# Edge records in two arrays, with the first 32 slots of each tile filled first, and keys and fields made in chunks of 120 columns

## The chip, the cores and the metric

One core of one Trainium2 chip runs the whole kernel in one launch. The metric is the device time in microseconds (us) of that core. The kernel is one program; its trace shows five engines: PE (matmul), DVE (vector), ACT (scalar), POOL (GpSimd) and SP (which issues transfers). "PEld" is PE's weight load. The core has 16 DMA engines that all transfers share. Transfers can be issued from the queues of SP and ACT, and from POOL, which issues the indirect ones.

## The reference, cut to what matters

A graph of 6250 nodes with 64 features, and 206250 directed edges sorted by target (100000 drawn edges in both directions, and one loop on each node). Four layers follow each other, each behind a layer norm and a ReLU, with a residual sum:

```python
h = relu(layernorm(x)); x = x + attention(h, edges)            # softmax over each node's edges, then a layer norm
h = relu(layernorm(x)); x = x + graph_conv(h, edges)           # sum over neighbours, scaled by degree
h = relu(layernorm(x)); x = x + message_net(h, edge_attr_64)   # two MLPs an edge, both directions
h = relu(layernorm(x)); x = x + gated_gnn(h, edge_type_4)      # 4 steps: sums by edge type, a GRU cell
```

All four sum over the same edges, so the kernel sorts the edges once into dense tiles and uses the tiles in all layers.

## The kernel before, in words

**Tiles and slots.** Nodes are padded to 49 blocks of 128 (`NB`), taken in 7 groups of 7 (`NG`, `GB`). A tile belongs to one group of target blocks and one source block, and a fiftieth tile of each group takes what a loop-laden diagonal pair has too much: `NC` = 50, so 350 tiles. A tile has `W` = 896 slots, 128 for each of its seven target blocks. Each slot holds a record of 70 floats (280 B): six fields and 64 edge features. All slots lie in the DRAM array `rec_d`; behind them it has one place an edge for those that find no room ("aside"). A slot's number is built from the pair of blocks (`base`) and the edge's rank within its pair, which counts on through all columns of edges. Slots that get no edge must hold -1 in their first four fields and zeros, so the array is filled before any record is written.

**Preparation (lines 189 to 251).** Edges lie as 128 partitions x 1620 columns (`EC`). The keys `dst`, `src` and the type are loaded whole. ACT issues seven fills of `rec_d` (line 215), each over 128 partitions. Meanwhile DVE makes from the keys: block numbers `bd` and `bs`, the fields `cf`, the pair's `key`, and `base`. PE turns `key` and `bd` into rows, stored in `row_d`. Then `pre_norm` makes `h` for the first layer.

**Sorting (`order`, to 2387 us in the trace).** Columns are taken in 162 groups of ten (`G`). The order of instructions on PE, ACT, DVE and SP is the one written out (`manual_schedule`). In iteration i: `load(i + 2)` issues three loads on SP, rows of keys `kr` (line 308), rows of block numbers `br` (line 310) and edge features into `rec` (line 312); `count(i + 1)` counts pairs on PE; `room_of(i + 1)` spreads what is left of each pair to the edges, after `br` is in; `settle(i)` works out rank and slot `pos` on DVE and then POOL issues ten indirect writes, one a column of 128 records (line 359). There are nine buffers for `rec` and ten for `pos`. Between these lie the projections of the first layer for iterations 0 to 13 (`projected`, with stores `q_d` and `v_d` on SP), and the attention scores after (`weights`, with a store on ACT).

**What reads the records.** The building of tiles (its own `load`, line 547: a tile's records `r`, and the scores `e`) makes count matrices `ak_d`; the message net (its `load`, line 928) reads the records again, beside rows `lid_d` and a table `pc`. A tile's records come as 128 partitions of 7 records, partition p holding the slots of rank p. When building ends a group, it stores 350 list rows to `lid_d` in writes of 128, 128 and 94 rows (line 631). A list of edges without room is worked off only if there are any.

Of the kernel before, what the change touches and what calls it, by code (L numbers as in the profile page):

```python
# [8 lines left out]
F32 = mybir.dt.float32  # L9
F32R = mybir.dt.float32r  # L10
F16 = mybir.dt.float16
# [3 lines left out]
I32 = mybir.dt.int32  # L15
AF = mybir.ActivationFunctionType
OP = mybir.AluOpType
AX = mybir.AxisListType

P = 128  # L20
D = 64
K = 4
# [4 lines left out]
class Plan:  # L27
# [7 lines left out]

    def __init__(self, n_nodes, n_edges, gb=7, group=10):
        self.N, self.E = n_nodes, n_edges
        nb = -(-n_nodes // P)
        self.NG = -(-nb // gb)
        self.GB = -(-nb // self.NG)  # L40
        self.NB = self.NG * self.GB
        self.NC = self.NB + 1
        self.NP = self.NB * P
        self.W = self.GB * P
        self.NSLOT = self.NG * self.NC * self.W
        self.G = group
        self.EC = -(-n_edges // (P * group)) * group
        self.EP = self.EC * P
        assert self.NB <= P and self.NB * self.NB <= 4094
        assert self.NSLOT + self.EP < 1 << 24 and K * self.NP < 1 << 24  # L50
        assert self.G * self.NB <= 512 and 512 < self.W <= 1024 or self.NG == 1
# [3 lines left out]
def gnn_stack(ctx: ExitStack, tc: tile.TileContext, pl: Plan, a: dict, out: bass.AP):  # L55
    nc = tc.nc
    NB, NC, NG, GB, W = pl.NB, pl.NC, pl.NG, pl.GB, pl.W
# [40 lines left out]
    nc.sync.dma_start(x, a["x"].rearrange("(b p) d -> p b d", p=P))  # L98
# [3 lines left out]
    rec_d = dram.tile([pl.NSLOT + pl.EP, RW], F32, name="rec_d")  # L102
    rec_v = rec_d[: pl.NSLOT, :].rearrange("(t p j) r -> t p j r", p=P, j=GB)
# [9 lines left out]
    e_d = dram.tile([NG * NB, P, W], F32, name="e_d")  # L113

# [18 lines left out]
    def pre_norm(pool):  # L133
        normalize(h, x, pool)
        nc.vector.tensor_scalar(h, h, 0.0, None, op0=OP.max)
# [46 lines left out]
    with ExitStack() as st:  # L182
# [3 lines left out]


        cf = sp.tile([P, EC, RF], F16, name="cf")
        nc.vector.memset(cf[:, :, 4], 1.0)
# [10 lines left out]
        nc.vector.tensor_scalar(minus, ident[:NB, :NB], -1.0, None, op0=OP.mult)  # L200

        with tc.tile_pool(name="prep", bufs=1) as pp:
            keys = {}
            for n in ("dst", "src", "ety"):
                keys[n] = pp.tile([P, EC], I32, name="k_" + n)
                nc.sync.dma_start(keys[n], a[n])

            many = max(f for f in (1, 2) if NC % f == 0)
            fill = sp.tile([P, many * GB, RW], F32, name="fill")
            nc.vector.memset(fill, 0.0)  # L210
            nc.vector.memset(fill[:, :, 0:4], -1.0)
            fill_v = rec_d[: pl.NSLOT, :].rearrange("(p i j) r -> p i (j r)", p=P, j=many * GB)
            per = NC // many
            for i in range(NG):
                nc.scalar.dma_start(fill_v[:, i * per : (i + 1) * per, :],
                                    fill.rearrange("p j r -> p (j r)")[:, None, :]
                                    .to_broadcast([P, per, many * GB * RW]))
            ti = pp.tile([P, EC], I32, name="ti")
            bf = pp.tile([P, EC], F32, name="bf")
            for n, b in (("dst", bd), ("src", bs)):  # L220
                nc.vector.tensor_scalar(ti, keys[n], 7, None, op0=OP.arith_shift_right)
                nc.vector.tensor_copy(b, ti)
            nc.vector.tensor_copy(bf, bd)
            for f, n in ((0, "dst"), (1, "src")):
                nc.vector.tensor_scalar(ti, keys[n], P - 1, None, op0=OP.bitwise_and)
                nc.vector.tensor_copy(cf[:, :, f], ti)
            for f, m, s in ((3, P - 1, 1), (5, 1, 0)):
                nc.vector.tensor_scalar(ti, keys["dst"], m, s, op0=OP.bitwise_and, op1=OP.arith_shift_right)
                nc.vector.tensor_copy(cf[:, :, f], ti)
            nc.vector.scalar_tensor_tensor(cf[:, :, 2], keys["ety"], float(P // 2), cf[:, :, 3],  # L230
                                           op0=OP.mult, op1=OP.add)
            nc.vector.tensor_scalar(cf[:, :, 5], cf[:, :, 5], 255.0, 1.0, op0=OP.mult, op1=OP.add)
            nc.vector.scalar_tensor_tensor(key, bd, float(NB), bs, op0=OP.mult, op1=OP.add)
            nc.vector.tensor_scalar(key, key, -float(NB * NB // 2), None, op0=OP.add)

            with tc.tile_pool(name="rowps", bufs=2, space=PSUM) as ps:
                for c0 in range(0, EC, P):
                    n = min(P, EC - c0)
                    pt = ps.tile([P, 2, P], F32, name="pt")
                    nc.tensor.transpose(pt[:n, 0, :], key[:, c0 : c0 + n], ident)  # L240
                    nc.tensor.transpose(pt[:n, 1, :], bf[:, c0 : c0 + n], ident)
                    rt = pp.tile([P, 2, P], F16, name="rt", bufs=3)
                    nc.vector.tensor_copy(rt[:n], pt[:n])
                    nc.sync.dma_start(row_d[:, c0 : c0 + n, :].rearrange("k t e -> t k e"), rt[:n])

            grp = pp.tile([P, EC], F32, name="grp")
            nc.vector.tensor_scalar(grp, bd, float(GB), None, op0=OP.is_ge)
            for k in range(2, NG):
                nc.vector.scalar_tensor_tensor(grp, bd, float(k * GB), grp, op0=OP.is_ge, op1=OP.add)
            nc.vector.scalar_tensor_tensor(base, bs, float(W), bd, op0=OP.mult, op1=OP.add)  # L250
            nc.vector.scalar_tensor_tensor(base, grp, float(NC * W - GB), base, op0=OP.mult, op1=OP.add)
# [10 lines left out]
        with tc.tile_pool(name="l0i", bufs=1) as wk:  # L262
            pre_norm(wk)

        sw = s2.enter_context(tc.tile_pool(name="sortw", bufs=3))
        ps = s2.enter_context(tc.tile_pool(name="sortps", bufs=2, space=PSUM))

# [34 lines left out]
        nc.gpsimd.iota(aside, pattern=[[1, G]], base=pl.NSLOT, channel_multiplier=EC,  # L302
# [22 lines left out]
        def settle(i, kr, rec, pr):  # L325
# [15 lines left out]
            nc.vector.scalar_tensor_tensor(pf, r, -float(GB), base[:, gs], op0=OP.mult, op1=OP.add)  # L341

            t1 = sw.tile([P, G], F32, name="t1")
            nc.vector.tensor_scalar(t1, bs[:, gs], -float(W), float((NB - 1) * W), op0=OP.mult, op1=OP.add)
            nc.vector.scalar_tensor_tensor(t1, r, -float(P), t1, op0=OP.is_le, op1=OP.mult)
            nc.vector.tensor_tensor(pf, pf, t1, op=OP.add)

            room = sw.tile([P, G], F32, name="room")
            nc.vector.tensor_tensor(room, bd[:, gs], bs[:, gs], op=OP.is_equal)
            nc.vector.tensor_scalar(room, room, -float(P - 1), -float(P), op0=OP.mult, op1=OP.add)  # L350
            ov = over[:, gs]
            nc.vector.tensor_tensor(ov, r, room, op=OP.is_le)
# [5 lines left out]
            for t in range(G):  # L358
                s = nc.gpsimd.indirect_dma_start(  # L359
                    out=rec_d, out_offset=bass.IndirectOffsetOnAxis(ap=pos[:, t : t + 1], axis=0),  # L360
                    in_=rec[:, t, :], in_offset=None)
                tc.declare_no_dep(s.ins, group="records", reason="each edge has its own slot")
                tc.add_to_no_dep_group("records", s.ins)

        def projected():

            for k, n0 in enumerate(range(0, pl.NP, 512)):
                n = min(512, pl.NP - n0)
                s = slice(n0, n0 + n)
                b0, nb = n0 // P, n // P  # L370
                hT = hTs[k % 2]
# [40 lines left out]
        def order():  # L412
            groups = EC // G
            ahead = [load(k) for k in range(min(2, groups))]
# [26 lines left out]
            for i in range(groups):  # L441
                share = scored(i)
                next(share, None)
                if i + 2 < groups:
                    ahead.append(load(i + 2))
                kr, _, rec = ahead.pop(0)
                if i + 1 < groups:
                    count(i + 1)
                next(share, None)
                nxt = room_of(i + 1, ahead[0][1]) if i + 1 < groups else None  # L450
                settle(i, kr, rec, pr)
                for _ in share:
                    pass
                pr = nxt
# [78 lines left out]
    with ExitStack() as st:  # L533
# [11 lines left out]
        def load(g, c):  # L545
            r = wk.tile([P, GB, RW], F32, name="r", bufs=4)
            nc.sync.dma_start(r, rec_v[g * NC + c])
            e = None
            if c < NB:
                e = wk.tile([P, W], F32, name="e", bufs=4)  # L550
                nc.sync.dma_start(e, e_d[g * NB + c])
            return r, e
# [320 lines left out]
    with ExitStack() as st:  # L873
# [4 lines left out]
        with ExitStack() as s1:  # L878
# [46 lines left out]
            def load(g, ci):  # L925
                t = g * NC + ci
                r = wk.tile([P, GB, RW], F32, name="r", bufs=3)
                nc.sync.dma_start(r, rec_v[t])
# [490 lines left out]
```

## Time and profile before

| | us |
|---|---|
| median of 10 runs | 9700.97 |
| lowest and highest | 9691.37, 9713.13 |
| the profiled execution's own time | 9684.43 |
| its span, first to last instruction | 9682.6 |
| first, 161st and last record write start | 250.38, 470.76, 2386.95 |
| building of tiles and the first layer's sum | 2387 to 3851 |
| message net, main loop | 4100 to 6910 |
| gated layer and end | 6910 to 9682 |

Over the span PE is busy 83%, DVE 77%, ACT 59%, POOL 30%, and the DMA engines move 1948.57 MB, 201 GB/s. The shares are means over stages with different limits; the windows of a stage say what limits it. A row of a window lists PE, PEld, DVE, ACT and POOL busy with their counts, then the granted PE clock, the mean busy share of the 16 DMA engines and the GB/s. Times of a row in the timeline are the start and the length; behind them stand engine, line, operation, what it writes and reads, and in brackets how long the engine was idle before and what ended that.

### The profile page before, as it was taken

What the parts mean: (1) busy time and instruction counts of PE and PEld (TensorE: products, weight loads), DVE (VectorE), ACT (ScalarE), POOL (GpSimd) and SP (SyncE); (2) the same over time, 40 slices, a digit from 0 to 9 for tenths busy, and PEclk for the clock granted to TensorE, in tenths of its full rate; (3) what the DMA queues carried; (4) which work ended last, traced back from release to release, by engine and by line L of the source; (5) the groups of instructions that cost most, each with busy time, mean ns of one, the idle gap of its engine ahead of it and who ended that gap; (6) DMA issues with size and microseconds to landing.
All of it is one profiled execution on the core that took longest, in us unless ns stands there. A gap on an engine that the chain in (4) does not pass through costs nothing. (4 is left out here: it accounts for less than half of the span.)

```text
span 9682.6 us, 146718 instructions
## 1 busy us (share of the span) xinstructions
PE 8048.1 (83%) x47524; PEld 6441.2 (67%) x47524; DVE 7486.0 (77%) x17172; ACT 5681.2 (59%) x8738; POOL 2877.2 (30%) x3651
## 2 busy tenths in 40 slices
PE   0564455453999999679999999999989999999999
PEld 0333333331444444568999999999768888888888
DVE  3697787774999998856777777777568888888888
ACT  0122122121666665546777777777568888888887
POOL 0777777776333332022222222222110000000000
PEclk9566666666999998879999999999989999999999
DMA  9565555554888886544444444444257777777777
GB/s 383 161 192 176 170 171 172 173 173 133 283 283 283 283 277 233 166 147 155 138 145 142 137 143 141 138 145 131 91 181 261 244 251 260 236 255 259 238 260 241
DMA packets 1035148, 1948.57 MB, mean 201 GB/s; under 512 B 327021, under 2 KB 579668, under 8 KB 1034214
## 3 DMA queue, kind: packets, MB, share of 16 engines
q1 hardware_dynamic: 748436, 1287.54, 41.4%
q10 hardware_dynamic: 224658, 564.27, 16.9%
q0 software_dynamic: 61248, 87.08, 2.7%
q8 instruction: 377, 6.18, 0.3%
q14 instruction: 429, 3.51, 0.1%
HBM read 1433.65 MB, written 504.81 MB: 200 GB/s over the span
## 5 line engine op out<-in xcount | busy, mean ns | idle before, releaser
L813 PE MATMUL ph<-mr,t 128*128 128x512 f32 x10976 | 2313.8, 370 | 9.6 <-DVE mr L799 8.1
L799 DVE CAST mr<-m 128x896 fp32r<-128x896 uint8 x3293 | 1954.0, 625 | 350.7 <-PE ph L813 244.4
L813 PEld LDWEIGHTS ph<-mr,t 128*128 128x128 f32 x10976 | 1991.2, 188 | 267.7 <-DVE mr L799 13.2
L797 ACT CAST mr<-m 128x896 fp32r<-128x896 uint8 x2195 | 1963.5, 940 | 309.1 <-PE ph L813 254.2
L359 POOL DMA_INDIRECT rec_d<-rec,pos x1620 | 1632.6, 1008 | 753.8 <-issue 437.2
L1062 DVE SCALAR_TENSOR_TENSOR m<-ph,m 128x512 fp32r<-128x512 f32 x1400 | 872.8, 623 | 423.0 <-ACT m L1061 390.6
L1078 POOL TENSOR_TENSOR acc_r<-acc_r,prc 128x128 f32<-128x128 f32 x784 | 610.8, 779 | 1799.4 <-ACT prc L1076 1768.7
L1061 ACT ACTIVATE m<-ph 128x512 fp32r<-128x512 f32 x1400 | 763.3, 545 | 572.3 <-PE ph L1054 530.7
L409 ACT ACTIVATE e<-e 128x896 f32<-128x896 f32 x343 | 323.9, 944 | 1244.7 <-DVE rec L357 310.7
L1054 PE MATMUL ph<-pc,st 128*128 128x256 f32 x4802 | 1008.1, 291 | 0.0
L1054 PE MATMUL ph<-qb,dt 128*128 128x256 f32 x4900 | 989.7, 284 | 0.0
L1054 PE MATMUL ph<-wc,eat 128*128 128x256 f32 x4900 | 988.8, 283 | 0.0
L599 ACT CAST ak<-pa 128x512 uint16<-128x512 f32 x1372 | 696.2, 534 | 387.7 <-PE pa L593 333.6
L1054 PEld LDWEIGHTS ph<-qb,dt 128*128 128x128 f32 x4900 | 762.0, 191 | 0.0
L1054 PEld LDWEIGHTS ph<-wc,eat 128*128 128x128 f32 x4900 | 758.7, 190 | 0.0
L1054 PEld LDWEIGHTS ph<-pc,st 128*128 128x128 f32 x4802 | 746.7, 192 | 8.1 <-DVE m L1062 6.3
L593 PE MATMUL pa<-kd,s 128*128 128x256 f16 x2401 | 687.6, 286 | 21.7 <-DVE kd L575 21.7
L1071 PE MATMUL pr<-m,so 128*128 128x260 f32 x2450 | 653.4, 285 | 22.1 <-ACT prc L1076 22.1
L293 PE MATMUL pc<-os,od 128*49 128x441 bf16 (+4 forms) x1619 | 374.1, 393 | 338.3 <-DVE os L270 337.7
L402 PE MATMUL pst<-qs,kt 128*128 128x512 f32 x1372 | 533.6, 533 | 135.3 <-DMA qs<-q_d 92.7
L1066 PE MATMUL pf<-m,do 128*128 128x256 f32 x2450 | 644.3, 281 | 0.0
L322 PE MATMUL pr<-y,dt 49*128 49x49 f16 x1620 | 90.1, 209 | 643.7 <-ACT y L296 598.9
(277 smaller groups left out, 13543.4 us busy)
## 6 DMA issues: line engine op xcount, KB each, us to landing
m<-ak_d SPq DMA_DIRECT2D x1372, 448.0 KB
r<-rec_d SPq DMA_DIRECT2D x700, 245.0 KB
e_d<-e ACTq DMA_DIRECT2D x343, 448.0 KB
e<-e_d SPq DMA_DIRECT2D x343, 448.0 KB
ak_d<-ak ACTq DMA_DIRECT2D x343, 448.0 KB
pc<-p_d SPq DMA_DIRECT2D x343, 256.0 KB
rec_d<-fill ACTq DMA_DIRECT2D x7, 12250.0 KB
rowst<-lid_d ACTq DMA_DIRECT2D x350, 224.0 KB
```

The source lines that it names most:

```text
L359: s = nc.gpsimd.indirect_dma_start(out=rec_d, out_offset=bass.IndirectOffsetOnAxis(ap=pos[:, t : t + 1], axis=0), in_=rec[:, t, :], in_off ...
L593: nc.tensor.matmul(pa, l_[:, j, :], r_[:, j, :], start=j % 2 == 0 and n == 0, stop=n + 1 == len(pairs), skip_group_check=True)
L599: nc.scalar.copy(ak2[:, :, (j + 1 - n) * HP : (j + 1) * HP].rearrange("p k (n q) -> p n k q", n=n), pa2[:, :n])
L797: nc.scalar.copy(m, src_t)
L799: nc.vector.tensor_copy(m, src_t)
L813: nc.tensor.matmul(ph[:, o : o + n], parts(c, k), r[:, o : o + n], start=(c == 0 and k == 0), stop=(c == NB - 1 and k == kk - 1))
L1054: nc.tensor.matmul(o, l_, r_, start=(q == 0 and j == j0), stop=(q == 5), skip_group_check=True)
L1061: nc.scalar.activation(mh, ph4, AF.Relu)
L1062: nc.vector.scalar_tensor_tensor(ml, ph4, 0.0, mh.bitcast(F32), op0=OP.max, op1=OP.subtract)
L1066: nc.tensor.matmul(pf[:, j], v["do"][:, j, :], m[:, j - j0, 0, : 2 * MSG], start=(ci == 0 and j % 2 == 0), stop=(ci == NB), skip_group_che ...
L1071: nc.tensor.matmul(pr, v["so"][:, j, :], m[:, j - j0, 1, :], start=(c is None or j == 0), stop=(c is None or j == GB - 1))
L1078: nc.gpsimd.tensor_tensor(acc_r[:, cb, :], acc_r[:, cb, :], prc[:, k * MSG : (k + 1) * MSG], op=OP.add)
```

## The change

- `rec_d` now has the places aside first and behind them two arrays of all slots. A record of rank under 32 (`R0`) goes to the first array, any other to the second; the fiftieth tile is all in the second.
- The fill comes in parts, with tiles on the outermost dimension (128, 128 and 94 of the 350): first the slots of rank under 32 in the first array (`fill_first`, three writes on ACT), then the others of the second array (`fill_others`), one write at the start of each of iterations 0 to 12: four quarters for each of the three sets of tiles, and the part of the fiftieth tiles.
- Groups 0 to 15 (`LEAD`, 160 columns) write to a slice of `rec_d` that ends with the first array; an edge of rank 32 or more would go aside there. From group 16 on the writes may go to all of `rec_d`. In the data no edge of the first 160 columns has a rank above 29.
- Keys and fields are made in 14 chunks of up to 120 columns: chunk 0 ahead of the loop, chunk k + 1 with its loads in iteration 12k + 1 and the rest in 12k + 3. The first norm is made in seven pieces as `projected` needs them.
- Both later loops load a tile's records with two transfers, 32 and 96 partitions (`load_records`).

```diff
+        self.R0 = P // 4
+        self.LEAD = max(1, self.EC // group // 10)
...
-    rec_d = dram.tile([pl.NSLOT + pl.EP, RW], F32, name="rec_d")
-    rec_v = rec_d[: pl.NSLOT, :].rearrange("(t p j) r -> t p j r", p=P, j=GB)
+    rec_d = dram.tile([pl.EP + 2 * pl.NSLOT, RW], F32, name="rec_d")
+    rec_p = [rec_d[pl.EP + k * pl.NSLOT : pl.EP + (k + 1) * pl.NSLOT, :] for k in range(2)]
+    rec_v = [r.rearrange("(t p j) r -> t p j r", p=P, j=GB) for r in rec_p]
+    rec_f = [r.rearrange("(t s) r -> t (s r)", s=W) for r in rec_p]
...
+    def load_records(r, t, ci):
+        if ci == NB:
+            nc.sync.dma_start(r, rec_v[1][t])
+        else:
+            nc.sync.dma_start(r[:R0], rec_v[0][t][:R0])
+            nc.sync.dma_start(r[R0:], rec_v[1][t][R0:])
...
+        many = 2
+        fill = sp.tile([P, many * GB * RW], F32, name="fill")
...
+        def fill_up(to, f):
+            n = to.shape[0]
+            to = to.rearrange("t (i e) -> t i e", e=many * GB * RW)
+            f.dma_start(to, fill[:n, None, :].to_broadcast(list(to.shape)))
+        def fill_first():
+            for t0 in range(0, NT, P):
+                fill_up(rec_f[0][t0 : min(NT, t0 + P), : R0 * GB * RW], nc.scalar)
+        def fill_others():
+            step = (P - R0) // 4 * GB * RW
+            for t0 in range(0, NT, P):
+                for q in range(4):
+                    o = R0 * GB * RW + q * step
+                    fill_up(rec_f[1][t0 : min(NT, t0 + P), o : o + step], nc.scalar)
+                    yield
+            fill_up(rec_p[1].rearrange("(g t s) r -> g t (s r)", t=NC, s=W)[:, NB, : R0 * GB * RW], nc.scalar)
+        fill_first()
...
-            fill_v = rec_d[: pl.NSLOT, :].rearrange("(p i j) r -> p i (j r)", p=P, j=many * GB)
-            per = NC // many
-            for i in range(NG):
-                nc.scalar.dma_start(fill_v[:, i * per : (i + 1) * per, :],
-                                    fill.rearrange("p j r -> p (j r)")[:, None, :]
-                                    .to_broadcast([P, per, many * GB * RW]))
...
+            if i < pl.LEAD:
+                nc.vector.tensor_scalar(ov, r, -float(R0), None, op0=OP.is_le)
+            else:
...
+                nc.vector.tensor_scalar(t1, r, -float(R0), float(pl.NSLOT), op0=OP.is_le, op1=OP.mult)
+                nc.vector.tensor_tensor(pf, pf, t1, op=OP.add)
...
-                    out=rec_d, out_offset=bass.IndirectOffsetOnAxis(ap=pos[:, t : t + 1], axis=0),
+                    out=rec_d[: pl.EP + pl.NSLOT, :] if i < pl.LEAD else rec_d, out_offset=...
...
+            keys = [load_keys(0)]
+            nc.sync.dma_start(x, a["x"].rearrange("(b p) d -> p b d", p=P))
+            prepare(0, keys.pop())
+            others = fill_others()
...
             for i in range(groups):
+                k, at = divmod(i, CH // G)
+                if k + 1 < len(chunks):
+                    if at == 1:
+                        keys.append(load_keys(k + 1))
+                    elif at == 3:
+                        prepare(k + 1, keys.pop())
+                next(others, None)
```

`prepare` does for 120 columns what the removed lines did for 1620, operation by operation, with its row store on SP; `load_keys` issues three loads on SP; `first_norm` does `pre_norm` for seven blocks at a time.

## The prediction

> **What bounds the kernel now.** I read the busy slices and the groups on the page first, then windows of the part that changes, then the timeline and the waits there. The change touches the sorting stage (to 2387 us) and the loads of records in two later stages. On the page, the scatters are 1620 indirect DMAs issued by POOL; the last starts at 2386.95 us, and the next stage reads what they wrote.
>
> ```profile
> L359 POOL DMA_INDIRECT rec_d<-rec,pos x1620 | 1632.6, 1008 | 753.8 <-issue 437.2
> ```
>
> From group 16 (scatter 160) on, one scatter starts every 1.313 us: 1008 ns busy and 0.30 us of "issue", in which POOL waits for nothing. The window says the same: 1471 us busy plus 1460 x 0.30 = 438 us make 1909 of its 1916 us. DVE has 490 us to spare in it, PE more. POOL sets the pace there, so what counts is when POOL begins. The columns are: window and length, then PE, PEld, DVE, ACT and POOL busy (count), PE clock, DMA share, GB/s.
>
> ```profile
> 10.00:249.00 239.00, 25.57 (x106) 14.28 (x106) 81.05 (x94) 6.41 (x11) 0.00 (x0) 0.95 1.02 390
> ...
> 470.80:2387.00 1916.20, 943.88 (x4312) 595.80 (x4311) 1426.31 (x5653) 381.93 (x475) 1471.32 (x1460) 0.65 0.52 169
> ```
>
> Up to 249 us the 16 DMA engines are full (share 1.02, 390 GB/s, so 24.4 GB/s an engine) with the fill: 7 x 12250 KB = 87.8 MB. ACT is held while issuing it, and the first scatter starts as it lands.
>
> ```profile
> 7.62 191.72 ACTq L215 DMA_DIRECT2D rec_d<-fill  x7
> ...
> 250.38 1.16 POOL L359 DMA_INDIRECT rec_d<-rec,pos  x1 [248.81 <-DMA br<-row_d]
> ```
>
> The releaser named here (br) is not it: the transfer records show the last fill packet at 248.8 us. In the first 160 scatters the pace is 1.378 us (470.76 - 250.38 over 160), a group of ten 13.8 us, and 14.4 over groups 4 to 11 (302.97 to 417.86 us).
>
> Two further views decide this case. SP's waits:
>
> ```profile
> SPq L310 <- DMA rec_d<-fill: 17.1, 1, 17.1
> ```
>
> A load of block rows (br) that has nothing to do with the fill waited for it. The trace shows why: issues from SP and ACT take eight semaphores in turn, and each waits until the transfer eight issues earlier has landed. And three writes of the later list rows (lid_d), two of 128 rows and one of 94, up to where other packets join; columns: length, PE clock, DMA share, GB/s:
>
> ```profile
> 2596.39:2596.78 0.39, 1.00 0.77 168
> 2597.93:2598.32 0.39, 1.00 0.77 168
> 2599.32:2599.99 0.67, 0.50 0.15 34
> ```
>
> The 94-row write, though smaller (47 against 64 KB), runs at a fifth of the rate. Its whole length is 1.57 us against 0.39, and in the transfer records a 128-row write ends with sixteen 4-byte packets, the 94-row one with two (3840.06 and 3840.07 us in the last group, where nothing else runs): it used two engines.
>
> **The change, part by part.** *The fill.* There are 350 tiles, and the new fills put tiles on the outermost dimension in pieces of 128, 128 and 94. The bytes hardly change. First part: 62,720 B a tile, so two writes of 8.03 MB and one of 5.90 MB. The rest: 47,040 B a tile in quarters, so eight writes of 6.02 MB, four of 4.42 MB, and a last one of 7 tiles (0.44 MB). A 128-tile piece runs at 390 GB/s: 20.6 us and 15.4 us. For a 94-tile piece there are two readings of the rows: by rate, a fifth of 390 (79 GB/s); by the end packets, two engines at 24.4 (48.8 GB/s). Small packets keep engines only partly busy, so the rate understates the gap for 3920 B packets; I take two engines: 121 us for the first part's piece, 90.6 us for each of the four others. The other reading gives 75 and 56 us, 46 + 138 = 184 us less in all; it stays as the lower end.
>
> *Start.* The first fill issues at about 8 us as now, its packets from 10. Two engines then have 41 + 121 us of fill and some 8 us of x and keys: it lands near 180 us. The first scatter needs all of it; group 0's keys, rank and columns are long done by then, but its record load is the eighth issue after the 94-tile piece and waits for it, so the first scatter comes near 185 us. Now 250: 65 us gained.
>
> *Groups 0 to 15.* Each of iterations 0 to 12 begins with a further fill on ACT. Per group the other traffic keeps the engines busy 0.47 (windows between 300 and 420 us) x 14.4 = 6.8 us. Fills 0 to 7: 8 x (15.4 + 6.8) = 178 us, to 358. Fills 8 to 11 on two engines: 4 x (90.6 + 6.8) = 390, to 748; with about two more groups of traffic, 762. The other 14 engines idle, and nothing slips past: fill i has the semaphore that the br load of iteration i+1 takes eight issues later, ACT is held while it issues, and SP's loads of records and keys queue behind. So groups wait too: the br load for group 14 goes out when fill 11 has landed, group 13 is settled after it on DVE, and its scatters start some 13 us later; groups 13 to 15 then take 39 us. Group 16, which may write everywhere and must wait for all fills, starts at 762 + 13 + 39 = 814 us, against 470.8: 343 us late. The fill is no longer the start's price but that of group 16.
>
> *From group 16 on* the pace is POOL's as now, so the 343 us stay to the end.
>
> *Keys and fields.* Removed ahead of the scatters: DVE's work (81 us of the first window with the norm), all under the fill. Added: 14 chunks of some 28 operations. At 128x1620 most of these took 1.0 to 2.9 us, at 128x10 the small ones take 0.17; at 120 columns I take 0.25, so 7 us a chunk, 98 in all. Also two more operations of 0.17 us a group, 50 us over 146 groups, and the norm in seven steps of about 5 us. The cover is DVE's 490 us and the nine record buffers by which it may run ahead of POOL; without cover it would be 98 + 50 us. In the held-up stretch it lies under the fills. Three more key loads and one row store for each chunk pass through SP, at 0.3 to 0.4 us an issue; SP waits for fills far longer. I take 0.
>
> *Record loads in two.* 686 more issues on SP, 0.32 to 0.43 us each, in front of the e and pc loads in their queues. In the building of tiles SP waits 886 us for PE to free e, in the messages stage 2271 us for DVE to free r; loads go out up to three blocks ahead. Bounds: 0, and 686 x 0.4 = 274 us if each were exposed; a gain is excluded, as bytes and packets stay. I take 0, nearest to SP's idle time.
>
> [...]
>
> **Sum.** The profiled run took 9684.4 us for a span of 9682.6; the median of the runs is 9701.0, 16.6 above it. 9684.4 + 343 = 10027, on the median 10044. By the rate reading it would be 159 us late, 9860.
>
> **Rivals.** *The fills run on all engines (faster).* The 94-tile pieces have another shape than the lid_d rows (3920 B packets, a repeated source), and could spread. Then the first fill lands at 75 us, the first scatter comes near 100 (x lies ahead of the row store on SP), iterations cost 15.4 + 6.8 = 22 us, 12 of them end at 340, and group 16 starts at 392: 79 us gained, 9622. Against it: the end packets. It decides where group 16 begins before 470.8, that is where the 94-tile pieces (23.6 MB, 483 us in my sum) need under 140 us: 168 GB/s, seven engines. Chance 0.09.
>
> *Early scatters wait for every fill queued ahead of them.* The slice to which the first 160 scatters are confined may not be told apart from the array filled beside it. Then fill and scatters of a group follow each other: 13 us more for each of 12 fills, group 16 at about 970, 10200. The diff makes the slice for this very purpose; chance 0.06.
>
> *The loads in two are exposed* in the two later stages, at up to 274 us on top of the main case. The SP waits speak against it; 0.04 for most of it.
>
> *It comes out even*, two effects cancelling within 0.2% (20 us, about what a measurement of this kernel can tell from no change): 0.02.
>
> The main case, group 16 held by the two-engine fills, has 0.79. Its own range: the engines' fill time alone with nothing added and group 16 straight behind, 10 + 41 + 121 + 123 + 362 = 657 plus two groups, 684 us, gives 9914; iterations of 30 us for fills 0 to 7, 20 us of other traffic beside each later one and twice the final 52 us make 814 + 62 + 53 + 52 = 981, so 10211. I set 9860 (the rate reading) to 10200, which leaves out the rival on the faster side and the upper part of the exposed loads. Slower has 0.79 + 0.06 + 0.04 = 0.89, the same 0.02, faster 0.09.
>
> **What would show it.** Right: first scatter near 185 us; fills of a 94-tile piece with a DMA share near 0.13 plus other traffic, some 90 us apart on ACT; SP's longest waits for rec_d<-fill; 160 scatters with long gaps until about 814 us, then 1.31 us a scatter to about 2730; later stages as long as now (1464 and 2810 us). Wrong: a DMA share near 1 throughout the fills and group 16 before 470 us; or a later stage that grew.

## The result, and the profile after

The changed kernel takes 9993.61 us (median of 8 runs, 9992.25 to 10006.02) against 9699.61 (28 runs of before over all comparisons with it): ratio 1.0308, 95% interval 1.0299 to 1.0317, so 294 us slower. Its profiled run took 9990.62 us for a span of 9988.8. The span grew by 306 us; 12 of that are in which run was profiled, since the one of before lay about 15 us below its median and this one 3 below.

On the page, the scatters' line is the same in busy time. Only the idle time has grown, by 299 us, of which "issue" has no more than before:

```profile
L426 POOL DMA_INDIRECT rec_d<-rec,pos x1620 | 1622.2, 1001 | 1053.2 <-issue 434.8
```

The windows show three regimes. The columns are window, length, PE, PEld, DVE, ACT and POOL busy (count), PE clock, DMA share, GB/s.

```profile
60.00:160.00 100.00, 0.00 (x0) 0.00 (x0) 0.00 (x0) 0.00 (x0) 0.00 (x0) 1.00 0.13 52
185.00:350.00 165.00, 63.95 (x269) 38.22 (x269) 81.54 (x310) 18.35 (x37) 79.04 (x80) 0.51 0.93 339
437.00:530.00 93.00, 7.59 (x38) 4.20 (x39) 9.92 (x40) 2.41 (x5) 8.56 (x10) 0.52 0.19 67
640.00:700.00 60.00, 0.00 (x0) 0.00 (x0) 0.00 (x0) 0.00 (x0) 0.00 (x0) 0.50 0.13 51
768.30:2676.00 1907.70, 993.16 (x4390) 617.86 (x4388) 1561.75 (x6303) 386.84 (x481) 1462.32 (x1459) 0.63 0.54 172
```

Rows one and four are whole stretches in which no compute engine does anything and the DMA engines stand at a share of 0.13, 51 to 52 GB/s: two sixteenths are 0.125. Row two, with the 128-tile pieces, has the engines nearly full. Row three is one 94-tile piece with one group of ten scatters beside it. Row five is POOL's pace again, 1.308 us a scatter, with DVE's 1426 us grown to 1562 by the moved work and still 346 short of the window.

The timeline of ACT's queue has the same in its issues. They are start and length; a long one is ACT's queue held at an issue while the piece before it goes out.

```profile
45.03 0.27 ACTq L210 DMA_DIRECT2D rec_d<-fill  x1
...
46.84 115.75 ACTq L210 DMA_DIRECT2D rec_d<-fill  x1
...
326.29 0.27 ACTq L210 DMA_DIRECT2D rec_d<-fill  x1
...
349.52 74.06 ACTq L210 DMA_DIRECT2D rec_d<-fill  x1
...
428.08 87.11 ACTq L210 DMA_DIRECT2D rec_d<-fill  x1
...
522.12 85.87 ACTq L210 DMA_DIRECT2D rec_d<-fill  x1
...
612.50 88.25 ACTq L210 DMA_DIRECT2D rec_d<-fill  x1
```

The short issues at 45.03 and 326.29 are the 94-tile pieces of the first part and of the first quarter; those at 349.52, 428.08 and 522.12 are the pieces of the other three quarters. Each of the long ones stands behind a 94-tile piece: 46.84 is a 128-tile quarter, 612.50 the part of the fiftieth tiles. In the transfer records the last end packets of the four quarters land at 436.6, 529.0, 621.3 and 713.6 us, two end packets each, where a 128-tile piece has sixteen; the last fill packet of all lands at 716.4. POOL's timeline shows what that makes of the scatters: the first one, the first of groups 9 and 10, and scatter 160 (group 16).

```profile
184.43 1.17 POOL L426 DMA_INDIRECT rec_d<-rec,pos  x1 [182.86 <-DMA rec_d<-fill]
...
434.78 0.96 POOL L426 DMA_INDIRECT rec_d<-rec,pos  x1 [66.73 <-DVE rec L424]
529.57 1.14 POOL L426 DMA_INDIRECT rec_d<-rec,pos  x1 [82.00 <-DVE rec L424]
768.25 1.02 POOL L426 DMA_INDIRECT rec_d<-rec,pos  x1 [0.30 <-issue]
```

Between 367 and 709 us groups 8 to 11 are each followed by a gap of 68 to 83 us. The releaser is DVE's copy into `rec`. What held DVE its own waits tell, here from 367 to 768 us (us in total, times, longest):

```profile
DVE q L193 <- ACT q L192: 238.0, 4, 82.2
DVE ln_r L326 <- ACT ln_v L324: 78.4, 1, 78.4
DVE dt L381 <- DMA br<-row_d: 9.9, 1, 9.9
```

So DVE waited 316 us for ACT's part of the first layer's projections, which stand between the groups in the written-out order, and ACT had its queue held at the next fill. One step, behind the issue at 428.08:

```profile
515.30 0.30 ACT L324 ACTIVATE ln_v<-ln_v,eps 128x7 f32<-128x7 f32 x1 [86.87 <-issue]
515.63 0.20 DVE L326 RECIPROCAL ln_r<-ln_v 128x7 f32<-128x7 f32 x1 [78.43 <-ACT ln_v L324]
```

SP was held beside it. Its longest waits to 760 us:

```profile
SPq L461 <- DMA rec_d<-fill: 322.8, 6, 82.8
SPq L458 <- DVE kt L456: 111.9, 1, 111.9
```

Line 461 is the store of `v_d`; 323 us of waits for a fill with which it shares nothing but one of the eight semaphores (the trace has number 106 on the fill issued at 326.29 and on the store at 437.16), and the loads for later groups stand behind it. But this did not hold groups 9 to 12: group 9's scatters start at 434.78, and the store goes out only at 437.16. In the step above the store goes out at 529.54, and ACT's copy that it writes had started only at 522.09; without the shared semaphore it could have gone some 7 us earlier. The only load that DVE waited for in this stretch is `br`, 9.9 us ahead of group 13. Both holds last as long as the same slow fill, and no run here has one without the other. The 111.9 us lie at the start, where the store of `q_d` waits for what DVE makes after ACT, and ACT's queue was held from 46.84 to 162.6 us.

### The profile page after: what moved, and what is told of

Same layout as the page of the kernel before. It is cut to its first block, busy times and chain, and to the rows that moved or that the text cites. A ratio compares the mean times of both kernels' runs of the same rounds, so it can differ in the third digit from the quotient of the medians.

```text
span 9988.8 us, 149281 instructions
## 1 busy us (share of the span) xinstructions
PE 8085.5 (81%) x47526; PEld 6459.5 (65%) x47526; DVE 7572.0 (76%) x17778; ACT 5685.5 (57%) x8745; POOL 2932.9 (29%) x3651
## 5 line engine op out<-in xcount | busy, mean ns | idle before, releaser
L355 PEld LDWEIGHTS <-od 128*49 128x49 bf16 x1619 | 224.0, 146 | 600.5 <-DVE od L332 365.1
```

The costliest lines, as they stand in the source:

```text
L355: nc.tensor.matmul(pc[:, t:, :], l_, r_.to_broadcast([r_.shape[0], G - t, NB]), start=k == 0, stop=k == len(terms) - 1, skip_group_check=True)
```

## The experiments

All twelve runs edit the changed kernel, but for one that edits the kernel before; three repeat an earlier edit on another chip. Kernels measured together ran on one chip beside the kernel before, and four chips were used. On two of them the kernel before itself took 10108 and 10118 us, so results there are read by their ratio (the last section has what differed).

### Are the two engines the cause?

The fill in pieces whose tile counts are 128, 80 and 14, and nothing else changed:

```diff
+        def even(t0):
+            n = min(NT - t0, P)
+            return [(a, b) for a, b in ((t0, t0 + n // 16 * 16), (t0 + n // 16 * 16, t0 + n)) if b > a]
...
-                fill_up(rec_f[0][t0 : min(NT, t0 + P), : R0 * GB * RW], nc.scalar)
+                for a0, a1 in even(t0):
+                    fill_up(rec_f[0][a0:a1, : R0 * GB * RW], nc.scalar)
```

and the same in `fill_others`.

> The changed kernel with each 94-tile piece of the fill split into 80 and 14 tiles (bytes, order and iterations unchanged). Two-engine theory (the 94-tile pieces run on two engines, and group 16 waits for them): first scatter near 80 us, DMA share near 1 all through the fills, twelve iterations of about 21 us, last fill near 335 us, group 16 some 52 us behind it at about 387 us, so 84 us ahead of the kernel before: about 9616 us. Rival one (early scatters wait for every fill queued ahead of them, whatever engines it uses): group 16 at about 12 x (21 + 13) + 80 + 52 = 540 us, 9770. Rival two (the moved keys and the loads in two cost the time): no change from 9994.

Measured, on one of the two slower chips: 10080.34 against 10108.19, ratio 0.9968 [0.9949, 0.9987]. First scatter 93.65 us, last fill packet 377, group 16 at 445.0 (80, 335 and 387 expected). Group 16 comes 323 us sooner than in the change; but the pace was 1.59 us a scatter there, so I ran the same kernel again on another chip.

> The even split once more (94 tiles as 80 and 14 in the first part and in the four quarters, nothing else touched), on another chip, because on the chip of the first call the sorting ran at 1.58 us a scatter in every kernel, so that POOL did not set the pace there. Theory (the two engines of the 94-tile pieces cost the start): first scatter near 94 us as in the first run, last fill packet by 380 us, group 16 at 400 to 445 us against 470.8 before, then 1.31 us a scatter, last scatter 25 to 70 us earlier than before, and with the 10 us that the loads in two cost, ratio 0.993 to 0.999. Rival (the fill is not the cause, the moved keys and fields or the two arrays are): group 16 stays behind 700 us and the ratio near 1.03.

9652.61 against 9710.22, ratio 0.9944 [0.9927, 0.9962]; first scatter 89.86, last fill packet 376.5, group 16 at 431.5, last scatter 2338.07 (48.9 earlier than before), pace 1.307. With the tiles dealt otherwise, the same change is 58 us faster instead of 294 slower. Its windows, where the change had 52 GB/s and nothing else:

```profile
60.00:100.00 40.00, 16.63 (x70) 9.93 (x69) 14.57 (x49) 7.68 (x13) 8.01 (x8) 1.00 1.00 300
100.00:250.00 150.00, 51.62 (x225) 31.02 (x225) 74.31 (x295) 13.85 (x28) 65.63 (x67) 1.00 1.02 360
...
431.60:2338.00 1906.40, 986.42 (x4390) 614.41 (x4388) 1559.98 (x6303) 387.00 (x481) 1461.66 (x1459) 0.63 0.54 173
```

To part the start from the later fills, only the first part split evenly (`even` in `fill_first` alone).

> Only the first part's 94-tile piece is split into 80 and 14; the four later ones stay. Two-engine theory: the first scatter moves from 184 to about 80 us, and the two engines lose 121 - 15 = 106 us of work, so the last fill lands near 610 us in place of 716, group 16 starts near 662, and the time is about 9994 - 106 = 9888 us. If only the start counted and the later fills were hidden, group 16 would move by 0 or by the whole gap and the later fills' 92 us steps would vanish; if the later pieces alone set the time, 9994.

10338.91 against 10108.19 on the same chip as the first run, two runs, ratio 1.0215 [1.0167, 1.0264]: first scatter 93.61, last fill packet 632 (610 expected), group 16 at 693.7 (662). The start is 91 us earlier than in the change, and group 16 still comes 223 us later than the 470.8 of before (both on other chips): the four late pieces cost more than the early start brings, as the steps of some 92 us in the change's trace had it.

### Do more engines bring more?

Pieces of 50 tiles, seven to a part, and halves in place of quarters (14 late fills in place of 13):

```diff
-            for t0 in range(0, NT, P):
-                fill_up(rec_f[0][t0 : min(NT, t0 + P), : R0 * GB * RW], nc.scalar)
+            for t0 in range(0, NT, NC):
+                fill_up(rec_f[0][t0 : min(NT, t0 + NC), : R0 * GB * RW], nc.scalar)
...
-            step = (P - R0) // 4 * GB * RW
+            step = (P - R0) // 2 * GB * RW
```

> The fill in seven pieces of 50 tiles, the later part in two halves each (14 writes, one an iteration): a middle dose. [...] If a remainder piece were slow for another reason (its place as the last piece, the address it writes to), all pieces here would run on 16 engines at 390 GB/s and the time would be as in the even split, about 9616.

10391.21, ratio 1.0253 [1.0211, 1.0295]: ten end packets a piece, where 128 tiles have sixteen and 94 two, so not 16 engines; but packets of 0.20 to 0.26 us instead of 0.16, last fill packet at 737 us. Ten engines at the 24.4 GB/s each of the kernel before would be, as an estimate, 244 GB/s; the window of this run, shown below, has 143. That was on a slower chip; so again on another one.

> The fill in pieces of 50 tiles (ten end packets a piece in the first call), once more, on another chip. Theory (number of engines alone, 24.4 GB/s each): 244 GB/s while the first part runs, 22 MB in 90 us, first scatter at 105 to 115 us, 65.8 MB of the rest in 270 us and other traffic, last fill packet near 430, group 16 at 480, ratio 1.001 to 1.005. Rival (on ten engines the packets themselves are slower, as the 0.21 to 0.26 us of the first call against 0.16): last fill packet past 600 us, group 16 past 650, ratio above 1.018.

9991.56 against 9710.22, ratio 1.0288 [1.0270, 1.0305], the rival's case: first scatter 159.7, last fill packet 721.8, group 16 at 767.3 us. Ten engines ended as late as two. The mean fill packet took 227 ns against 162 in the change, and the windows stop at 165 GB/s with the share at 0.59, ten engines busy but slow. That is not the whole delay: a later piece (4.7 MB) takes 28 us at 165 GB/s, and from 482 to 644 us the pieces were issued some 40 us apart. What the other 12 us are no run shows.

```profile
60.00:120.00 60.00, 0.57 (x10) 0.43 (x9) 0.00 (x0) 1.86 (x2) 0.00 (x0) 1.00 0.59 165
```

What makes the packets slow? The pieces are read from the first n partitions of one constant tile, n being the number of tiles. So a further run reads the same 50-tile pieces from every second partition:

```diff
-            f.dma_start(to, fill[:n, None, :].to_broadcast(list(to.shape)))
+            f.dma_start(to, fill[: n * (P // n) : P // n, None, :].to_broadcast(list(to.shape)))
```

> The fill in pieces of 50 tiles as in the run before it (9991.56 us, packets of 0.20 to 0.25 us on ten engines, 120 to 185 GB/s), with one thing changed: the 50 partitions of the constant tile that the pieces are read from are every second one (0, 2, to 98) and no longer 0 to 49. Written bytes, their places, the engines and the order stay. Theory (packets are slow because many engines read from few neighbouring partitions): packets back near the 0.16 us of the pieces of 128 tiles, 244 GB/s on ten engines, first scatter at 105 to 125 us, last fill packet at 400 to 470, group 16 at 440 to 520 us, ratio 0.997 to 1.006. Rival (the slowness is on the side of the writes, by the distance of a tile's slots in DRAM or by ten engines as such): packets stay at 0.20 to 0.25 us, group 16 near 767 us, ratio 1.029. [...]

10242.49 against 10118.21, ratio 1.0125 [1.0108, 1.0142], between the two: first scatter 135.3, last fill packet 590, group 16 at 629.0, mean packet 191 ns. The windows of the two 50-tile kernels on the slower chips, read from neighbouring partitions first, from spread ones second:

```profile
60.00:100.00 40.00, 0.00 (x0) 0.00 (x0) 0.00 (x0) 0.00 (x0) 0.00 (x0) 1.00 0.57 143
```

```profile
60.00:100.00 40.00, 0.57 (x10) 0.43 (x9) 0.00 (x0) 1.86 (x2) 0.00 (x0) 1.00 0.62 221
```

143 to 221 GB/s, with written bytes, engines and order untouched. The two ran on two chips of the slower kind; with the same kernel (neighbouring partitions) a slower chip and another one gave packets of 232 and 227 ns, so the chip is not what took them to 191. Where these pieces are read from counts too, and it is somewhat over half of the excess over 162 ns. The rest is open. Why neighbouring partitions give slower packets no run shows. The 221 GB/s come near the estimate of 244 for ten engines.

### Do the other parts cost nothing?

All fills ahead of the first scatter, in even pieces, no early groups (`LEAD = 0`, `fill_others` worked off behind `fill_first`).

> The even split, but with all fills issued ahead of the loop and no early groups (all groups go the way of group 16): what is left of the change is the chunked keys and norm and the loads in two. Theory: 88 MB at 390 GB/s from 10 us, with x and keys beside it: first scatter near 250 us as before, and the moved work lies under POOL's pace of 1.31 us a scatter, so 9700 us within 20. Rival two (moved work exposed): up to 98 + 50 us for keys and slots and up to 274 us for the loads, 9720 to 10070.

10248.59, ratio 1.0121 [1.0086, 1.0156]; the first scatter came at 325.9 and not near 250, because the last pieces ran at a fraction of the rate (141 against 402 GB/s in the repeat, below). Again on the other chip.

> All fills ahead of the first scatter in even pieces, no early groups, so that what is left of the change is the keys and fields in chunks, the two arrays and the loads in two. Theory (the moved work lies under POOL's pace): first scatter at 250 to 330 us, depending on how the pieces of 14 tiles run, 160 scatters at 1.31 to 1.38 us behind it, pace 1.31 us from group 16 on, and the ratio follows from the first scatter plus 10 us: 1.001 for 250 us, 1.009 for 330. Rival (98 + 50 us of moved DVE work exposed): pace 1.40 us from group 16 on, some 130 us more at the last scatter, ratio 1.014 to 1.023.

9803.80 against 9710.22, ratio 1.0092 [1.0074, 1.0110]. The windows show why the fill took 68 us more: pieces of 128 tiles first, then those of 80 and 14.

```profile
120.00:200.00 80.00, 0.00 (x0) 0.00 (x0) 0.00 (x0) 0.00 (x0) 0.00 (x0) 1.00 1.02 402
260.00:300.00 40.00, 7.35 (x46) 4.62 (x46) 4.62 (x10) 5.55 (x8) 0.00 (x0) 0.99 0.70 141
```

Behind the first scatter (318.16 us) the first 160 took 250 us, where before had 220: 30 us. POOL's waits for DVE's copy into `rec` are 44.5 us there against 13.7 in before's, 31 more, and DVE was busy 180 us against 154, so I put the 30 us down to the moved work. From group 16 on the pace is 1.306, so the rival's 130 us are not there. Where no fill covers it the moved work costs 30 us, and nothing after.

The loads in two, put alone into the kernel before:

```diff
-            nc.sync.dma_start(r, rec_v[t])
+            if ci == NB:
+                nc.sync.dma_start(r, rec_v[t])
+            else:
+                nc.sync.dma_start(r[:P // 4], rec_v[t][:P // 4])
+                nc.sync.dma_start(r[P // 4:], rec_v[t][P // 4:])
```

(in both loops.)

> The kernel before with one edit: a tile's records are loaded in two transfers of 32 and 96 partitions from its one array. Theory (loads go out up to three blocks ahead, SP waits for buffers): 9700 us within 10, below 0.1%. Rival (the 686 further issues of about 0.4 us are exposed, or they hold each other through the eight semaphores): up to 9974 us; the profiled run of the changed kernel was 17 us longer than the kernel before after the last scatter, and if the loads were the cause this run would show about 9715.

9718.59 (11 runs) against 9708.71 (15), ratio 1.0010 [1.0001, 1.0019]: about 10 us, and between 1 and 18. In its profiled run the building of tiles is as long as before to 0.2 us, so what there is would lie behind it.

### A version that beats both

A larger first part, so that more groups may start before the second array is filled (in the first 240 columns no edge has a rank above 44): `R0 = 48`, `LEAD = 24`, even split.

> The even split with the first 48 slots of each tile filled first and open to the first 240 columns (24 groups), whose ranks stay below 45. Theory: first part 32.9 MB, first scatter near 105 us; later fills of 12.9 us beside 6.8 us of other traffic, 12 iterations of 20 us, done near 345 us, before group 24 comes at POOL's own pace (105 + 24 x 13.8 = 436 us; before, scatter 240 came near 578 us): 142 us ahead, about 9558 us. If DMA load still sets the early groups' pace: group 24 near 500 us, 9620.

9668.33 against 9708.71, ratio 0.9963 [0.9949, 0.9977]: the rival's mechanism, at a smaller gain than even it had. Group 24 came at 540.2, against 577.7 before and the 500 that the rival had. First scatter at 126.99; the first 120 scatters took 254 us, where before had 167, with the DMA engines full:

```profile
127.00:381.00 254.00, 99.24 (x421) 59.03 (x420) 121.89 (x485) 26.41 (x54) 119.55 (x120) 1.00 0.95 293
```

So the next one halves each late fill and spreads them over 24 iterations, with the fiftieth tiles' part ahead:

```diff
-            step = (P - R0) // 4 * GB * RW
+            step = (P - R0) // 8 * GB * RW
+            fill_up(rec_p[1].rearrange("(g t s) r -> g t (s r)", t=NC, s=W)[:, NB, : R0 * GB * RW], nc.scalar)
...
-                for q in range(4):
+                for q in range(8):
...
-            fill_up(rec_p[1].rearrange("(g t s) r -> g t (s r)", t=NC, s=W)[:, NB, : R0 * GB * RW], nc.scalar)
```

> As the run with 48 slots in the first part and 24 early groups, but the fill of the second array in eighths, one in each of iterations 0 to 23, and the fill of the fiftieth tiles' first slots ahead of them. Theory (in that run the first twelve groups were held because each iteration's fill of 22 to 30 us kept the engines full and SP's loads behind it): an eighth is 2.5 MB, 6.4 us at 390 GB/s, and with 6.8 us of other traffic as long as a group at POOL's 13.1 us, so groups follow at 14 to 16 us from the first scatter at 105 to 127 us; group 16 at 340 to 380 us against 470.8, 9585 to 9625 us, ratio 0.987 to 0.992. Rival (what holds the early groups is the number of issues and the projections' stores, not the size of a fill): group 16 near 434 us as there, ratio 0.996.

9638.02 against 9710.22, ratio 0.9931 [0.9914, 0.9948]; group 16 at 381.9 against 433.8. The first 120 scatters took 191 us against 254, so the size of an iteration's fill was most of what held the groups. It falls short of the 9585 to 9625 expected: the fill ends at 500.0, and group 24, the first that must wait for all of it, starts at 511.1. The first scatter came at 132.8 and the pieces of 80 and 14 still ran slowly. Last, with 64 and 30 in their place, each read from spread partitions:

```diff
-            return [(a, b) for a, b in ((t0, t0 + n // 16 * 16), (t0 + n // 16 * 16, t0 + n)) if b > a]
+            m = n if n == P else P // 2
+            return [(a, b) for a, b in ((t0, t0 + m), (t0 + m, t0 + n)) if b > a]
```

> The version with 48 slots in the first part, 24 early groups and eighths (9638.02 us), with 94 tiles as 64 and 30 where it had 80 and 14, and each piece read from partitions spread over the constant tile (every second for 64, every fourth for 30). Theory (the pieces of 80 and 14 tiles ran at 100 to 290 GB/s because they read from neighbouring partitions): first part of 33 MB at 350 to 390 GB/s, first scatter at 100 to 115 us against 132.8, no stretch of the fill with packets over 0.20 us, last fill packet some 40 to 80 us before the 500 us of that run, group 16 at 340 to 365 us, 9600 to 9625 us, ratio 0.989 to 0.992. Rival (the engines are full in any case and the pieces of 14 cost nothing that lasts): group 16 at 380 us and ratio 0.993 again.

10015.58 against 10118.21, ratio 0.9898 [0.9878, 0.9918], on a slower chip. First scatter 111.5, last fill packet 483.5, group 16 at 378.7, although a scatter at full pace takes 1.57 us there and not 1.31. The end of the first part, in the version with 80 and 14 and in this one:

```profile
90.00:110.00 20.00, 0.57 (x10) 0.43 (x9) 0.00 (x0) 1.86 (x2) 0.00 (x0) 1.00 0.91 231
```

```profile
80.00:100.00 20.00, 2.42 (x17) 1.37 (x17) 1.98 (x4) 4.02 (x5) 0.00 (x0) 1.00 1.02 386
```

The theory's start holds; its 340 to 365 us for group 16 can't be judged on this chip. Two of its signs fail: the last fill packet lands 16 us before the 500 us of the run before it, and not 40 to 80, and from 100 to 110 us the mean packet is 214 ns. The mean fill packet is 172 ns against 193; the split and the partitions that are read changed together, so no run tells what each did.

## Why the prediction was right, and where it was off

- **94-tile pieces on two engines**: right. Share 0.13 and 51 to 52 GB/s alone, two end packets. That they are the cause is shown by the even split: the same change with 80 + 14 for 94 goes from 294 us behind the kernel before to 58 us ahead of it (9993.61 and 9652.61, ratios 1.0308 and 0.9944). But the count of engines is not the rate: the rival's turning point, seven engines, was no good measure, for with ten the fill ended no earlier (last fill packet at 721.8 us, 716.4 in the change). The end packets counted were two for 94 tiles, ten for 50, seven for 7 and sixteen for 128; how the engines follow from other counts is not shown here. The packets of the `lid_d` rows are of 256 B in the trace of before, and sixteen engines stood at a share of 0.77 with them, at 1.02 with the fill's 3920 B: the rate of the rows understated the gap, as put.
- **First scatter** near 185: 184.43. It waited for the fill itself, which landed at 183. The record load of group 0, which I had waiting behind the fill's semaphore, had gone out at 23.0 us.
- **Fills 0 to 7** from 180 to 358: from 183 to 338.6, where the last of them lands, 156 us in place of 178.
- **Fills 8 to 11**: predicted 390 us, and 14 more for two groups of traffic; measured 338.6 to 713.6, 375 us. So 762 was 48 us too late. The term that was mis-sized is the other traffic: I charged 12 x 6.8 + 14 = 96 us of it, and from 183 to 713.6 us only 45 are not the fills' own time (8 x 15.4 + 4 x 90.6 = 486). The traffic itself was there: in the row of 437 to 530 us the engines are busy 0.19 x 93 = 17.7 us on average, 11.6 of it two engines' fill, which leaves 6. Yet a step took 92.3 us, 1.7 more than the fill alone. It did not keep off the two engines: the record load issued at 531.05 has 14 of its 16 semaphore counts by 535.9 us and the last two at 553.7. Why it lengthened the fill so little stays open.
- **What holds the groups**: this is where the account in the prediction does not fit. I had the load of block rows wait for the fill's semaphore, with SP's loads behind it, and named ACT's held queue only beside that. In the trace groups 9 to 12 wait for DVE, which waits 316 us for ACT, whose queue is held at the next fill. The semaphore's rule held (six waits, 322.8 us), with the store of `v_d` (line 461) as the instruction that waits, but from 367 us on it ends a wait of DVE only ahead of group 13, 9.9 us. That the effect, one group a fill, came out right owes something to luck: both holds last about one fill.
- **The tail**: predicted 13 us from fill 11 to group 13's scatters and 39 for groups 13 to 15, 52; measured 713.6 to 726.5 and on to 768.2, 13 and 42. Here the load of `br` is what the prediction said: it goes out at 715.05, and group 13 is settled after it.
- **Pace of POOL** unchanged at 1.313: 1.308, which gave 8 us back by the last scatter (289 late, group 16 being 297 late).
- **Keys and fields at 0**: right for this kernel as far as its sum shows; in the held-up stretch DVE stood waiting for ACT for 316 us. With no fill to cover it, where the most was put at 148 us, it cost 30: DVE has room from group 16 on in any case (1562 of 1908 us).
- **Loads in two at 0**: about 10 us, against bounds of 0 and 274, so nearly all is covered. From the last scatter to the end the changed kernel's trace is 17 us longer than before's, one of them in the building of tiles; 12 us of the two traces' difference lie in which run was profiled.
- **Rivals.** Fills on all engines: refuted by the share of 0.13. Early scatters waiting for every fill: refuted by the trace, since group 8's scatters start at 355.5 us while the fill that was issued ahead of them at 326.3 lands at 436.6. Loads in two exposed: about 10 us, at most 18.

So 343 predicted, 297 measured at group 16, 289 at the last scatter, 294 on the medians.

## What to carry to other kernels

Before a large transfer is cut, look at the count on its outermost dimension (here 128 ended with sixteen end packets, 50 with ten and 94 with two): a 94-row write of 1.57 us in the old trace, with its two end packets, told of 300 us in the new one. Then read what a slow transfer holds up. Here it was first the queue that issues the next one: ACT stood 74 to 88 us at an issue, and the engines that wait for ACT's results stood with it. Beside it, the issue that comes eight later waits for the shared semaphore, here up to 82.8 us. More engines alone need not help: where a constant tile is the source, spreading the partitions that it is read from gave 221 GB/s for 143.

## What the runs showed that I had not expected

- **Fill rates by piece** (mean packets from the transfer records): 128 tiles about 160 ns, 402 GB/s; 50 tiles on ten engines 227 ns, 165 GB/s; with pieces of 80 and 14 tiles, all fills ahead, 257 ns and 224 GB/s from 210 to 250 us, and 415 ns and 91 GB/s of fill from 280 to 300. Reading from spread partitions took 232 down to 191 ns (50 tiles). Over the whole fill of the last version the mean went from 193 down to 172, with 64 and 30 tiles for 80 and 14 besides.
- **The same kernel on other chips.** On two chips the kernel before took 10108 and 10118 us against 9700 to 9710. Only later kernels were profiled there; in them the scatters follow at 1.57 to 1.59 us instead of 1.31, 0.27 x 1460 = 394 us, nearly all of the 398 to 418 us between the medians of the kernel before. That it runs so there too is inferred. The even split on the slower chip and then on the other:

```profile
L432 POOL DMA_INDIRECT rec_d<-rec,pos x1620 | 1617.4, 998 | 1142.0 <-DVE rec L430 560.6
```

```profile
L432 POOL DMA_INDIRECT rec_d<-rec,pos x1620 | 1621.3, 1001 | 716.1 <-issue 437.7
```

A scatter takes as long, but POOL waits for DVE's copy there, and no longer sets the pace. ACT's waits in the slower sorting stage name a releaser that the trace doesn't show:

```profile
ACT y L364 <- remote: 208.5, 18, 15.8
```

What it is stays open. It means that work moved onto DVE in this stage, free on one chip, need not be free on the other.
